# Two graph layers on one core: one-hot rows made from PSUM in halves, a base read once, and row constants in PSUM

## The chip, the core and the metric

The kernel runs on one core of a Trainium2 chip. The core has five engines with a queue each: PE (TensorE, matrix products), DVE (VectorE), ACT (ScalarE), POOL (GpSimd) and SP (which only issues transfers here). An engine works through its queue in the order in which the instructions were put there, and waits for others by semaphores. The metric is the device time of one execution in microseconds (us); the kernel before has a median of 2407.45 us over three runs (2405.77 to 2409.37).

## What is computed

A graph of 6250 nodes with 128 features and 106,250 edges, sorted by destination. Two layers, each on a layer norm of its input and added to it. The first is an attention layer, the second a gated message layer:

```python
# layer 0 (h = relu(layernorm(x)))
m = leaky_relu(xl[src] + xr[dst] + edge_attr @ We, 0.2)
logits = m @ att
alpha = softmax of logits over the edges of each dst
out = segment_sum(xl[src] * alpha, dst)          # then gelu, batch norm
# layer 1 (h = relu(layernorm(x)))
em = relu(layer_norm(concat(h[src], h[dst]) @ msg_w + msg_b))
msgs = segment_sum(em * edge_weight, dst) / counts
h_new = relu(layer_norm(concat(h, msgs) @ upd_w + upd_b))
x = x + gate * h_new + (1 - gate) * h
```

## The kernel before

The edges are padded to 128 x 832 and cut into 104 blocks of 1024, eight tiles of 128 edges each. The edges of one block reach at most 126 consecutive destinations (the kernel tests that first, and has another path for graphs of which it isn't true). So a block s has a *base*, its first destination, and a *window* of 126 node rows from there on.

**Tables and setup.** A first stage makes the tables xl_d and xr_d in DRAM, one row per node. Then `fast()` (from L740) makes small per-edge columns. `dl_b` holds each edge's destination minus its block's base, a bf16 row of 1024 numbers per block with one block per partition; it is written to DRAM as `dl_d` (L794).

**The edge loops.** Two loops over blocks, one per layer (L1020 and L1286), stand under a manual schedule: each engine's queue has the instructions in the order of the program. A round s of either loop does, in this order:

- `load` (L851): SP fetches the window of block s+2 (126 rows of xr_d or b_d) into one of three tiles W, and `dlb`, the block's row of dl_d repeated on all 128 partitions (L856, 256 KB). The row to start from comes from `base_of` (L762), which reads the base into a register of SP.
- POOL issues eight indirect gathers (L196), one per tile of 128 edges, for the source rows of block s: `gl`. The first loop has ten such buffers, the second six.
- `spread` / `spread1`: PE spreads the window of block s+1 over its edges (`expand`, L867: 16 matmul instructions, from the one-hot tile `oht`) into PSUM.
- DVE adds gl to the spread rows of block s (L1033, L1298), ACT goes on with the sum (L1034; squares at L1303).
- For an older block u (u = s-7 in the first loop, s-1 in the second) DVE makes the one-hot `oh` of destinations by edges (L1040, L1309), from `iota_ps`, a constant row 0..127 held in PSUM.
- First loop: ACT scales gl of block u by its softmax weights into `glw` (L1049); DVE goes on with block s (L1051 to L1057). Second loop: DVE scales y of block u by its reciprocal deviation and the row mg_r (L1314, eight instructions) and adds the row mb_r (L1316), both rows in SBUF; ACT does the relu (L1317) and the edge weights (L1320) into `glw`.
- `one_hot_t` (L861): DVE makes `oht` of block s+2 in one instruction from dlb (L863), 1 where the partition's number is the edge's offset.
- PE sums the edges of block u by destination, `agg` (L1063, L1329, 16 matmul instructions); ACT copies the sums out in the next round, and `store` (L869) has SP write them to the window's rows in DRAM, for which it reads the base again.

Around this, generators are taken one step further per round: in the first loop `maxima` (L896, softmax maxima of four blocks, whose small transposes share one PSUM buffer with the tag "mx") and `nodes` (L949), in the second `nodes1` (L1202), which finishes 512 nodes in eight steps, with transposes in PSUM buffers "nt" and "nz" (L1226 to L1228, L1236 to L1240, L1264 to L1273). After both loops a tail finishes the last nodes.

In PSUM the spread rows have two buffers; iota_ps, the sums and the two others of each loop (mx and np, nt and nz) have one each.

Of the kernel before, what the change touches and what calls it, by code (L numbers as in the profile page):

```python
# [9 lines left out]
F32 = mybir.dt.float32  # L10
BF16 = mybir.dt.bfloat16
# [5 lines left out]
P = 128  # L17
# [31 lines left out]
def kernel(  # L49
# [691 lines left out]
    def fast():  # L741
# [4 lines left out]
        fs = fx.enter_context(tc.tile_pool(name="fstate", bufs=1))  # L746
        a_d = dram.tile([NP, D], F32, name="a_d")
        b_d = dram.tile([NP + P, D], F32, name="b_d")
        dl_d = dram.tile([NS, SE], BF16, name="dl_d")
        res0_d = [dram.tile([NP + P, W0], F32, name=f"res0_{i}") for i in range(2)]  # L750
        res1_d = [dram.tile([NP + P, WL], F32, name=f"res1_{i}") for i in range(2)]
        hT_sb = h_sb.rearrange("p t f -> p (t f)")
        xT_sb = x_sb.rearrange("p t f -> p (t f)")

        dl_c = fs.tile([P, NS, ST], F32, name="dl_c")
        ew_c = fs.tile([P, NS, ST], F32, name="ew_c")
        eac_c = fs.tile([P, NS, ST], F32, name="eac_c")
        fst_c = fs.tile([P, NS, ST], F32, name="fst_c")
        base_row = fs.tile([1, NS], I32, name="base_row")
        nc.sync.dma_start(base_row, flat(dst, [[1, 1], [SE, NS]]))  # L760

        def base_of(s):  # L762
            return nc.values_load(base_row[0:1, s : s + 1], engines=[mybir.EngineType.SP],
                                  min_val=0, max_val=NP - 1)


        kbrk = fs.tile([NBT, BT, P + 1], BF16, name="kbrk")
# [17 lines left out]
        with tc.tile_pool(name="col1", bufs=1) as p1, tc.tile_pool(name="rows", bufs=2) as rp, tc.tile_pool(  # L785
            name="ps_p", bufs=2, space=PSUM
        ) as ps_p:
            base_f = p1.tile([NS, 1], F32, name="base_f")
            V.tensor_copy(base_f, dst_r[:, 0:1])
            fr = rp.tile([NS, SE], F32, name="fr", tag="rows")  # L790
            V.tensor_scalar(fr, dst_r, base_f, None, op0=ALU.subtract)
            dl_b = p1.tile([NS, SE], BF16, name="dl_b")
            V.tensor_copy(dl_b, fr)
            nc.sync.dma_start(dl_d, dl_b)  # L794

            for w in Ws:
                nc.scalar.dma_start(w[WIN : WIN + 1], We)
                nc.scalar.dma_start(w[WIN + 1 : P], flat(br, [[0, 1], [1, D]]))
            for o in ohts:
                V.memset(o, 1.0)  # L800
            ends_i = p1.tile([1, 2, K], I32, name="ends_i")
            nc.scalar.dma_start(ends_i[:, 0, :], flat(dst, [[1, 1], [P, K]]))
            nc.scalar.dma_start(ends_i[:, 1, :], flat(dst, [[1, 1], [P, K]], P - 1))
            ea_r = rp.tile([NS, SE], F32, name="ea_r", tag="rows")
            nc.sync.dma_start(ea_r, flat(edge_weight1, [[SE, NS], [1, SE]]))
            for c, vec in ((bias_c, bias_out), (bng_c, bn_gamma), (bnb_c, bn_beta)):
                nc.scalar.dma_start(c, flat(vec, [[1, P], [1, 1]]))
            nc.scalar.dma_start(gb_c, flat(gate_b, [[0, P], [1, 1]]))
# [12 lines left out]
            ew_r = rp.tile([NS, SE], F32, name="ew_r", tag="rows")  # L821
            nc.sync.dma_start(ew_r, flat(edge_weight, [[SE, NS], [1, SE]]))
            columns(ps_p, ew_c, ew_r, "ctp")


            V.memset(kbrk[:, :, 0:1], 0.0)
            V.memset(kbrk[:, :, P : P + 1], 0.0)
            HB = 7
            for b in range(0, BT, HB):
                n = min(HB, BT - b)  # L830
                dst_n = p1.tile([NBT, HB, P], I32, name="dst_n")
                nc.sync.dma_start(dst_n[:, :n, :], flat(dst, [[P, NBT], [P * NBT, n], [1, P]], b * P * NBT))
# [12 lines left out]
        def zero(tables, n, i):  # L845

            for r in tables:
                nc.sync.dma_start(r.rearrange("(p k) f -> p (k f)", p=P)[:, i * 5 * n : (i + 1) * 5 * n],
                                  zt[:, : 5 * n])

        def load(pool, table, s, weights):  # L851

            w, oht = Ws[s % 3], ohts[s % 3]
            nc.sync.dma_start(w[:WIN], table[ds(base_of(s), WIN), :])
            dlb = pool.tile([P, SE], BF16, name="dlb")
            nc.sync.dma_start(dlb, flat(dl_d, [[0, P], [1, SE]], s * SE))  # L856
            if weights:
                nc.sync.dma_start(oht[WIN : WIN + 1, :], flat(edge_weight1, [[SE, 1], [1, SE]], s * SE))
            return w, dlb, oht

        def one_hot_t(w, dlb, oht):  # L861

            V.tensor_scalar(oht[:WIN, :], dlb[:WIN, :], iota_p[:WIN, :], None, op0=ALU.is_equal)  # L863

        def expand(ps, oht, w):
            for j in range(ST):
# [1 line left out]

        def store(agg, tables, s):  # L869
            nc.sync.dma_start(tables[s % 2][ds(base_of(s), WIN), :], agg[:WIN, :])  # L870

        def fetch(fin, tables, t0, n):

# [12 lines left out]
        with tc.tile_pool(name="e0", bufs=2) as ep, tc.tile_pool(  # L886
# [1 line left out]
        ) as op_, tc.tile_pool(name="e0m", bufs=2) as mp, tc.tile_pool(name="e0n", bufs=1) as np_, tc.tile_pool(  # L888
            name="ps_m", bufs=2, space=PSUM
        ) as ps_m, tc.tile_pool(name="ps_1", bufs=1, space=PSUM) as ps_1, tc.manual_schedule():  # L890
            iota_ps = ps_1.tile([P, P], F32, name="iota_ps")
            S.copy(iota_ps, iota_f)
            LAG = SB + 3
            gls, lgc, exm, wins, pss, aggs = {}, {}, {}, {}, {}, {}

# [103 lines left out]
                S.copy(xT_sb[:, t0 * P : (t0 + n) * P], tp[:, : n * P])  # L999

            def spread(s):
                w, _, oht = wins.pop(s)
                pss[s] = ps_m.tile([P, ST, D], F32, name="m_ps")
                expand(pss[s], oht, w)

# [9 lines left out]
            for s in range(2):  # L1015
                wins[s] = load(op_, xr_d, s, True)
            for s in range(2):
                one_hot_t(*wins[s])
            spread(0)
            for s in range(NS + LAG + 1):  # L1020
                u = s - LAG
# [15 lines left out]
                if 0 <= u < NS:  # L1037
                    b, q = divmod(u, SB)
                    oh = ep.tile([P, ST, P], F32, name="oh")
                    V.tensor_tensor(oh, over_tiles(iota_ps, ST), over_features(dl_c[:, u, :], ST),  # L1040
                                    ALU.is_equal)
                    glw = ep.tile([P, ST, W0], F32, name="glw")
                    V.tensor_copy(glw[:, :, D:], exm[b][:, q])  # L1043
                if u >= 1:
                    flush(u - 1)
                if 0 <= u < NS:
# [9 lines left out]
                        lgc[s // SB] = mp.tile([P, SB, ST], F32, name="lgc")  # L1056
                    V.tensor_add(lgc[s // SB][:, s % SB, :], lr, eac_c[:, s, :])  # L1057
                if s + 2 < NS:
                    one_hot_t(*wins[s + 2])
                if 0 <= u < NS:  # L1060
                    aggs[u] = ps_1.tile([P, W0], F32, name="agg_ps")
                    for j in range(ST):
# [115 lines left out]
        with tc.tile_pool(name="e1g", bufs=6) as gp, tc.tile_pool(name="e1", bufs=2) as ep, tc.tile_pool(  # L1178
# [1 line left out]
        ) as yp, tc.tile_pool(name="e1o", bufs=2) as op_, tc.tile_pool(name="e1s", bufs=1) as e1, tc.tile_pool(  # L1180
            name="ps_m1", bufs=2, space=PSUM
        ) as ps_m, tc.tile_pool(name="ps_11", bufs=1, space=PSUM) as ps_1, tc.manual_schedule():
            iota_ps = ps_1.tile([P, P], F32, name="iota_ps1")
            S.copy(iota_ps, iota_f)
            glws = [e1.tile([P, ST, WL], F32, name=f"glw1_{i}") for i in range(3)]
            for t in glws:
                V.memset(t[:, :, D : D + 1], 1.0)
# [2 lines left out]
            wins, pss, aggs, rss, ys = {}, {}, {}, {}, {}  # L1190

            def spread1(s):
                w, _, oht = wins.pop(s)
                pss[s] = ps_m.tile([P, ST, D], F32, name="y_ps")
                expand(pss[s], oht, w)

# [84 lines left out]
            for s in range(2):  # L1281
                wins[s] = load(op_, b_d, s, False)
            for s in range(2):
                one_hot_t(*wins[s])
            spread1(0)
            for s in range(NS + 2):  # L1286
                u = s - 1
# [19 lines left out]
                if 0 <= u < NS:  # L1307
                    oh = ep.tile([P, ST, P], F32, name="oh1")
                    V.tensor_tensor(oh, over_tiles(iota_ps, ST), over_features(dl_c[:, u, :], ST),  # L1309
                                    ALU.is_equal)  # L1310
                    yu = ys.pop(u)
                    ru = rss.pop(u)
                    for j in range(ST):
                        V.scalar_tensor_tensor(yu[:, j, :], yu[:, j, :], ru[:, j : j + 1], mg_r,  # L1314
                                               op0=ALU.mult, op1=ALU.mult)
                    V.tensor_tensor(yu, yu, over_tiles(mb_r, ST), ALU.add)  # L1316
                    S.activation(yu, yu, AF.Relu)  # L1317
                    glw = glws[u % 3]
                    for j in range(ST):
                        S.activation(glw[:, j, :D], yu[:, j, :], AF.Copy, scale=ew_c[:, u, j : j + 1])  # L1320
                if s + 2 < NS:
                    one_hot_t(*wins[s + 2])
                if s < NS:
                    V.reciprocal(rs, rs)
                    rss[s] = rs
# [59 lines left out]
```

## Time and profile before

| what | us |
|---|---|
| median of three runs | 2407.45 |
| the profiled execution | 2414.23 |
| its span, first to last instruction | 2412.4 |
| gathers of the first loop | from 71.6 to 1145.7 |
| gathers of the second loop | from 1256.8 to 2355.2 |
| POOL busy | 1699.7 |
| DVE busy | 1637.3 |
| PE busy | 1375.8 |
| ACT busy | 1276.6 |

A line of a group gives the code line, the engine, the operation, the tile written and those read, the shapes, the number of instructions, and behind the bar the busy time and the mean of one in ns, then the idle time of the engine ahead of them and what ended it. A row of the timeline gives the start in us from the span's start, the duration, the engine, the line and the operation; several instructions in a row are merged ("x8"), and the idle time ahead of the first stands in brackets with what ended it. In the chain of what ended last, "issue" is time in which an engine waited for nothing that the profile shows. PE's ends are modelled, so neighbours may overlap by a tenth or two.

### The profile page before, as it was taken

How to read it: one execution, taken by the hardware profiler on the slowest of the kernel's cores; microseconds unless marked ns; L12 is line 12 of the kernel's file. 1: busy time of each engine (PE TensorE's matmuls, PEld its weight loads, DVE VectorE, ACT ScalarE, POOL GpSimd, SP SyncE). 2: the span in 40 equal slices, each digit the busy share in tenths (PEclk: the TensorE clock that was granted, in tenths of full speed). 3: DMA queues.
4: the chain of work that ended last, by engine and by line, in shares of the span. 5: the costliest groups of instructions: out<-in, count | busy, mean ns of one | idle time of the engine just before them, and what ended most of it. 6: DMA issues, size and time to landing. Idle time of an engine off the chain costs nothing.

```text
span 2412.4 us, 30614 instructions
## 1 busy us (share of the span) xinstructions
PE 1375.8 (57%) x7692; PEld 1270.8 (53%) x7692; DVE 1637.3 (68%) x3597; ACT 1276.6 (53%) x4267; POOL 1699.7 (70%) x1703
## 2 busy tenths in 40 slices
PE   6446555556566556565484555555655655555553
PEld 3345555555555455565464555555555654555553
DVE  6666677677677667767445567677767768768765
ACT  5223343334344334344456676676676677667663
POOL 1677777777777777777057777777777777777770
PEclk9667887787878777777687677778777777777876
DMA  6743455443443433443142333343333333333331
GB/s 166 211 114 92 111 151 137 98 100 92 101 100 92 98 96 92 100 100 80 32 132 79 90 94 99 85 107 97 83 107 97 85 108 103 83 101 102 85 96 30
DMA packets 217496, 242.90 MB, mean 101 GB/s; under 512 B 41373, under 2 KB 158077, under 8 KB 217309
## 3 DMA queue, kind: packets, MB, share of 16 engines
q0 software_dynamic: 53792, 110.57, 19.7%
q1 hardware_dynamic: 160657, 130.00, 18.5%
q8 instruction: 64, 1.05, 0.2%
q14 instruction: 123, 1.01, 0.1%
q10 hardware_dynamic: 2860, 0.27, 0.1%
HBM read 197.43 MB, written 43.25 MB: 100 GB/s over the span
## 4 chain that ended last, share of the span: by engine, by line
POOL 44%; issue 18%; DMA 14%; DVE 13%; PE 7%; ACT 3%; SPq 0%; DVEq 0%; another core or an unknown queue 0%; ACTq 0%; POOLq 0%
POOL gl L196 44%; DMA gl<-xl_d,src_c 7%; DMA gl<-a_d,src_c 5%; DVE y L1314 2%; DVE m_ps L1033 2%; PE agg_ps L1063 2%; DVE y L1298 1%; DVE oh L1309 1%; PE agg_ps L1329 1%; DVE y L1316 1%; PE mm L255 1%; PE mm L1156 1%; ACT sq L1303 1%; DVE oh L1040 1%; DVE oht L863 1%
## 5 line engine op out<-in xcount | busy, mean ns | idle before, releaser
L196 POOL DMA_INDIRECT gl<-xl_d,src_c x832 | 820.9, 987 | 308.8 <-issue 229.8
L196 POOL DMA_INDIRECT gl<-a_d,src_c x832 | 845.2, 1016 | 260.7 <-issue 234.3
L1329 PE MATMUL agg_ps<-glw,oh 128*128 128x129 f32 x1664 | 363.9, 403 | 485.7 <-ACT glw L1320 439.7
L1329 PEld LDWEIGHTS agg_ps<-glw,oh 128*128 128x128 f32 x1664 | 336.3, 298 | 505.8 <-ACT glw L1320 505.8
L1063 PE MATMUL agg_ps<-glw,oh 128*128 128x130 f32 x1664 | 345.0, 389 | 386.3 <-DVE glw L1043 206.8
L1063 PEld LDWEIGHTS agg_ps<-glw,oh 128*128 128x128 f32 x1664 | 320.7, 288 | 404.1 <-ACT glw L1049 404.1
L1034 ACT ACTIVATE m_ps<-m_ps 128x1024 f32<-128x1024 f32 x104 | 104.8, 1008 | 573.6 <-DVE m_ps L1033 429.3
L1303 ACT ACTIVATE sq<-y 128x128 f32<-128x128 f32 x832 | 257.1, 309 | 275.8 <-DVE y L1298 252.4
L1033 DVE TENSOR_TENSOR m_ps<-m_ps,gl 128x1024 f32<-128x1024 f32 x104 | 128.1, 1232 | 299.9 <-DMA gl<-xl_d,src_c 273.7
L867 PE MATMUL m_ps<-W,oht 128*128 128x128 f32 x1664 | 259.8, 320 | 36.2 <-DVE oht L863 22.8
L867 PEld LDWEIGHTS m_ps<-W,oht 128*128 128x128 f32 x1664 | 243.8, 233 | 45.2 <-issue 22.3
L1320 ACT ACTIVATE glw<-y,ew_c 128x128 f32<-128x128 f32 x832 | 254.4, 389 | 3.4
L1049 ACT ACTIVATE glw<-gl,exm 128x128 f32<-128x128 f32 x832 | 254.3, 394 | 0.0
L1298 DVE TENSOR_TENSOR y<-y_ps,gl 128x1024 f32<-128x1024 f32 x104 | 126.8, 1220 | 187.8 <-DMA gl<-a_d,src_c 146.7
L867 PE MATMUL y_ps<-W,oht 128*128 128x128 f32 x1664 | 230.4, 298 | 13.2 <-DVE oht L863 9.0
L867 PEld LDWEIGHTS y_ps<-W,oht 128*128 128x128 f32 x1664 | 226.7, 218 | 13.8 <-issue 13.8
L1314 DVE SCALAR_TENSOR_TENSOR y<-y,rs,mg_r 128x128 f32<-128x128 f32 x832 | 227.3, 344 | 0.0
L863 DVE TENSOR_SCALAR oht<-dlb,iota_p 126x1024 f32<-126x1024 bf16 x208 | 159.3, 766 | 15.1 <-DMA dlb<-dl_d 15.0
L1303 ACT ACTIVATION_READ_ACCUMULATOR sq<-y 128x1 f32 x832 | 155.0, 186 | 0.0
L1051 DVE TENSOR_TENSOR m_ps<-m_ps,att 128x1024 f32<-128x1024 f32 x104 | 131.3, 1263 | 4.8 <-ACT m_ps L1034 4.6
L1317 ACT ACTIVATE y<-y 128x1024 f32<-128x1024 f32 x104 | 109.9, 1057 | 41.1 <-DVE y L1316 41.0
L1316 DVE TENSOR_TENSOR y<-y,mb_r 128x1024 f32<-128x1024 f32 x104 | 127.7, 1228 | 3.6
(251 smaller groups left out, 1610.7 us busy)
## 6 DMA issues: line engine op xcount, KB each, us to landing
dlb<-dl_d SPq DMA_DIRECT2D x208, 256.0 KB
gl<-xl_d,src_c POOLq DMA_INDIRECT x832
gl<-a_d,src_c POOLq DMA_INDIRECT x832
res<-agg SPq DMA_DIRECT2D x104, 64.0 KB
res<-agg SPq DMA_DIRECT2D x104, 63.5 KB
W<-xr_d SPq DMA_DIRECT2D x104, 63.0 KB
W<-b_d SPq DMA_DIRECT2D x104, 63.0 KB
res<-zt SPq DMA_DIRECT2D x20, 325.0 KB
```

The costliest lines, as they stand in the source:

```text
L196: GP.indirect_dma_start(out=dest, out_offset=None, in_=table, in_offset=bass.IndirectOffsetOnAxis(ap=idx, axis=0))
L863: V.tensor_scalar(oht[:WIN, :], dlb[:WIN, :], iota_p[:WIN, :], None, op0=ALU.is_equal)
L867: T.matmul(ps[:, j, :], oht[:, j * P : (j + 1) * P], w, start=True, stop=True)
L1033: V.tensor_tensor(ps, ps, gl[:, :, :D], ALU.add)
L1049: S.activation(glw[:, j, :D], glu[:, j, :D], AF.Copy, scale=exm[b][:, q, j, 1:2])
L1063: T.matmul(aggs[u], oh[:, j, :], glw[:, j, :], start=(j == 0), stop=(j == ST - 1))
L1298: V.tensor_tensor(y, pss.pop(s), gl, ALU.add)
L1303: S.activation(sq, y[:, j, :], AF.Square, accum_out=rs[:, j : j + 1])
L1314: V.scalar_tensor_tensor(yu[:, j, :], yu[:, j, :], ru[:, j : j + 1], mg_r, op0=ALU.mult, op1=ALU.mult)
L1316: V.tensor_tensor(yu, yu, over_tiles(mb_r, ST), ALU.add)
L1320: S.activation(glw[:, j, :D], yu[:, j, :], AF.Copy, scale=ew_c[:, u, j : j + 1])
L1329: T.matmul(aggs[u], oh[:, j, :], glw[:, j, :], start=(j == 0), stop=(j == ST - 1))
```

## The change

Three things, in one diff.

1. The offsets `dl_b` stay in SBUF; dl_d and the load of dlb are gone. `one_hot_t` now works on half a block (512 edges): PE multiplies a column of the identity, repeated 128 times (it picks the block's row of dl_b), with the half row, which puts the offsets on all partitions in a PSUM tile `dlp`; DVE makes the half of oht from it. dlp takes the one buffer "mx" in the first loop and "nt" in the second. The first half is put ahead of the older work of the round: in the first loop after the one-hot oh and the copy at L1043, in the second between L1309 and L1314. The second half stands where the one instruction stood.
2. The base of a block is read into SP's register once, and kept until `store`.
3. A helper `constants` puts rows into one PSUM tile: iota in the first loop, as before; iota, mg_r and mb_r in the second, where L1314 and L1316 read them from there.

```diff
+        dl_b = fs.tile([NS, SE], BF16, name="dl_b")
+        ident_b = fs.tile([P, P], BF16, name="ident_b")
+        V.tensor_copy(ident_b, ident)
...
+        bases = {}
+
         def base_of(s):
-            return nc.values_load(base_row[0:1, s : s + 1], engines=[mybir.EngineType.SP],
-                                  min_val=0, max_val=NP - 1)
+            if s not in bases:
+                bases[s] = nc.values_load(base_row[0:1, s : s + 1], engines=[mybir.EngineType.SP],
+                                          min_val=0, max_val=NP - 1)
+            return bases[s]
...
-            dl_b = p1.tile([NS, SE], BF16, name="dl_b")
             V.tensor_copy(dl_b, fr)
-            nc.sync.dma_start(dl_d, dl_b)
...
+        def constants(pool, *rows_):
+
+            n = 1 + len(rows_)
+            t = pool.tile([P, n * P], F32, name="cst")
+            for k, r in enumerate((iota_f,) + rows_):
+                S.copy(t[:, k * P : (k + 1) * P], r)
+            return [t[:, k * P : (k + 1) * P] for k in range(n)]
+
         def load(pool, table, s, weights):
 
             w, oht = Ws[s % 3], ohts[s % 3]
             nc.sync.dma_start(w[:WIN], table[ds(base_of(s), WIN), :])
-            dlb = pool.tile([P, SE], BF16, name="dlb")
-            nc.sync.dma_start(dlb, flat(dl_d, [[0, P], [1, SE]], s * SE))
             if weights:
                 nc.sync.dma_start(oht[WIN : WIN + 1, :], flat(edge_weight1, [[SE, 1], [1, SE]], s * SE))
-            return w, dlb, oht
-
-        def one_hot_t(w, dlb, oht):
-
-            V.tensor_scalar(oht[:WIN, :], dlb[:WIN, :], iota_p[:WIN, :], None, op0=ALU.is_equal)
+            return w, oht
+
+        def one_hot_t(pool, tag, s, k, w, oht):
+
+            es = slice(k * CH, (k + 1) * CH)
+            dlp = pool.tile([P, CH], F32, name="dlp", tag=tag)
+            T.matmul(dlp, ident_b[:NS, s : s + 1].to_broadcast([NS, P]), dl_b[:, es], start=True, stop=True)
+            V.tensor_scalar(oht[:WIN, es], dlp[:WIN, :], iota_p[:WIN, :], None, op0=ALU.is_equal)
```

The first loop:

```diff
             for s in range(2):
-                one_hot_t(*wins[s])
+                for k in range(2):
+                    one_hot_t(ps_1, "mx", s, k, *wins[s])
...
                     V.tensor_copy(glw[:, :, D:], exm[b][:, q])
+                if s + 2 < NS:
+                    one_hot_t(ps_1, "mx", s + 2, 0, *wins[s + 2])
                 if u >= 1:
                     flush(u - 1)
...
                 if s + 2 < NS:
-                    one_hot_t(*wins[s + 2])
+                    one_hot_t(ps_1, "mx", s + 2, 1, *wins[s + 2])
```

The second loop:

```diff
-            iota_ps = ps_1.tile([P, P], F32, name="iota_ps1")
-            S.copy(iota_ps, iota_f)
+            iota_ps, mg_ps, mb_ps = constants(ps_1, mg_r, mb_r)
...
                     V.tensor_tensor(oh, over_tiles(iota_ps, ST), over_features(dl_c[:, u, :], ST),
                                     ALU.is_equal)
+                if s + 2 < NS:
+                    one_hot_t(ps_1, "nt", s + 2, 0, *wins[s + 2])
+                if 0 <= u < NS:
                     yu = ys.pop(u)
                     ru = rss.pop(u)
                     for j in range(ST):
-                        V.scalar_tensor_tensor(yu[:, j, :], yu[:, j, :], ru[:, j : j + 1], mg_r,
+                        V.scalar_tensor_tensor(yu[:, j, :], yu[:, j, :], ru[:, j : j + 1], mg_ps,
                                                op0=ALU.mult, op1=ALU.mult)
-                    V.tensor_tensor(yu, yu, over_tiles(mb_r, ST), ALU.add)
+                    V.tensor_tensor(yu, yu, over_tiles(mb_ps, ST), ALU.add)
...
                 if s + 2 < NS:
-                    one_hot_t(*wins[s + 2])
+                    one_hot_t(ps_1, "nt", s + 2, 1, *wins[s + 2])
```

More of the change, by code (lines that the diff above doesn't have):

```diff
@@ L748, in fast @@
         b_d = dram.tile([NP + P, D], F32, name="b_d")
-        dl_d = dram.tile([NS, SE], BF16, name="dl_d")
         res0_d = [dram.tile([NP + P, W0], F32, name=f"res0_{i}") for i in range(2)]
@@ L870, in store @@
             nc.sync.dma_start(tables[s % 2][ds(base_of(s), WIN), :], agg[:WIN, :])
+            del bases[s]
         def fetch(fin, tables, t0, n):
@@ L890, in fast @@
         ) as ps_m, tc.tile_pool(name="ps_1", bufs=1, space=PSUM) as ps_1, tc.manual_schedule():
-            iota_ps = ps_1.tile([P, P], F32, name="iota_ps")
-            S.copy(iota_ps, iota_f)
+            (iota_ps,) = constants(ps_1)
             LAG = SB + 3
@@ L1001, in spread @@
             def spread(s):
-                w, _, oht = wins.pop(s)
+                w, oht = wins.pop(s)
                 pss[s] = ps_m.tile([P, ST, D], F32, name="m_ps")
@@ L1182, in fast @@
         ) as ps_m, tc.tile_pool(name="ps_11", bufs=1, space=PSUM) as ps_1, tc.manual_schedule():
-            iota_ps = ps_1.tile([P, P], F32, name="iota_ps1")
-            S.copy(iota_ps, iota_f)
+            iota_ps, mg_ps, mb_ps = constants(ps_1, mg_r, mb_r)
             glws = [e1.tile([P, ST, WL], F32, name=f"glw1_{i}") for i in range(3)]
@@ L1192, in spread1 @@
             def spread1(s):
-                w, _, oht = wins.pop(s)
+                w, oht = wins.pop(s)
                 pss[s] = ps_m.tile([P, ST, D], F32, name="y_ps")
@@ L1283, in fast @@
             for s in range(2):
-                one_hot_t(*wins[s])
+                for k in range(2):
+                    one_hot_t(ps_1, "nt", s, k, *wins[s])
             spread1(0)
```

## The prediction, made before the change was run

> **What bounds the kernel now.** I read the page first (busy shares, the chain that ended last, the costliest groups), then the spread of the gathers' durations, then the timeline of one round of each edge loop.
>
> ```profile
> span 2412.4 us, 30614 instructions
> PE 1375.8 (57%) x7692; PEld 1270.8 (53%) x7692; DVE 1637.3 (68%) x3597; ACT 1276.6 (53%) x4267; POOL 1699.7 (70%) x1703
> POOL 44%; issue 18%; DMA 14%; DVE 13%; PE 7%; ACT 3%; SPq 0%; DVEq 0%; another core or an unknown queue 0%; ACTq 0%; POOLq 0%
> L863 DVE TENSOR_SCALAR oht<-dlb,iota_p 126x1024 f32<-126x1024 bf16 x208 | 159.3, 766 | 15.1 <-DMA dlb<-dl_d 15.0
> ```
> ```profile
> L196 POOL DMA_INDIRECT gl<-xl_d,src_c x832: 940/944/1701, 71.6 to 1144.8; - x167
> L196 POOL DMA_INDIRECT gl<-a_d,src_c x832: 940/945/1954, 1256.8 to 2354.3; - x167
> ```
> The chain is mostly POOL's gathers and the 0.305 us between two of them ("issue"). 832 x (0.944 + 0.305) = 1039 us for a loop, 9.99 us for a round of eight; the loops' gathers take 1074 and 1098 us. POOL never waits for a buffer in either loop: its gaps are all 0.3 us. The rest is stretch: 820.9 - 832 x 0.944 = 35.5 us in the first loop, 845.2 - 785.4 = 59.8 in the second.
>
> ```profile
> 1517.74 1.74 POOL L196 DMA_INDIRECT gl<-a_d,src_c  x1 [0.30 <-issue]
> 1518.58 0.74 DVE L863 TENSOR_SCALAR oht<-dlb,iota_p 126x1024 f32<-126x1024 bf16 x1
> ```
> The gather that meets the one-hot of L863 ends 0.16 us after it, 0.80 late. Laying POOL's rows on DVE's: gathers over 0.96 us that overlap an L863 hold 30.2 us of the first loop's stretch and 48.6 of the second's; those that overlap only L1314 or L1316 hold 9.6.
>
> The other clock is the hand-over between engines. One round of the second loop and the head of the next:
>
> ```profile
> 1502.07 1.23 DVE L1298 TENSOR_TENSOR y<-y_ps,gl 128x1024 f32<-128x1024 f32 x1 [5.02 <-DMA gl<-a_d,src_c]
> 1503.21 1.21 DVE L1309 TENSOR_TENSOR oh<-iota_ps,dl_c 128x1024 f32<-128x1024 f32 x1
> 1504.35 2.18 DVE L1314 SCALAR_TENSOR_TENSOR y<-y,rs,mg_r 128x128 f32<-128x128 f32 x8
> 1506.56 1.22 DVE L1316 TENSOR_TENSOR y<-y,mb_r 128x1024 f32<-128x1024 f32 x1
> 1507.70 0.75 DVE L863 TENSOR_SCALAR oht<-dlb,iota_p 126x1024 f32<-126x1024 bf16 x1
> 1507.82 1.06 ACT L1317 ACTIVATE y<-y 128x1024 f32<-128x1024 f32 x1 [0.56 <-DVE y L1316]
> 1508.91 2.45 ACT L1320 ACTIVATE glw<-y,ew_c 128x128 f32<-128x128 f32 x8
> 1509.36 3.81 PE L1329 MATMUL agg_ps<-glw,oh 128*128 128x129 f32 x16 [7.27 <-ACT glw L1320]
> 1512.96 2.62 PE L867 MATMUL y_ps<-W,oht 128*128 128x128 f32 x16
> 1512.95 1.23 DVE L1298 TENSOR_TENSOR y<-y_ps,gl 128x1024 f32<-128x1024 f32 x1 [0.83 <-DMA gl<-a_d,src_c]
> 1515.22 2.18 DVE L1314 SCALAR_TENSOR_TENSOR y<-y,rs,mg_r 128x128 f32<-128x128 f32 x8
> ```
> See: each queue runs in program order, and the spread of the next window (L867) comes right behind the segment sums (L1329). Its result is first used by the L1298 of the round after, so today the ring STT (L1314) -> relu -> weights -> sums -> spread -> L1298 closes over two rounds. In the 1512.95 round DVE goes straight on from L1309 to L1314 while PE still spreads until 1515.6.
>
> **The change, part by part.**
> *Load of destinations gone:* 208 transfers of 256 KB, SP issues of 0.34 us, and the dl_d write. W and the gathers have the DMA engines at 35 to 43%, and POOL doesn't wait for landings: 0. L863's 15.0 us wait for dlb goes; DVE then waits for the gather instead (256 and 138 us of such waits): 0. If the cover were gone, 15 us.
> *Base read once:* a register read less on SP per round. SP's longest waits are for the flushed sums, it has no work late: 0; at worst a few tenths per round on a queue that idles most of it.
> *One-hot from PSUM:* two halves of 512 for one of 1024. No row shows a tensor-scalar of 512 from PSUM. From below, half of L863's 0.66 start-to-start, 0.33; from above, L984's scalar-tensor-tensor of 512 from PSUM, 0.744, of which the next instruction overlaps 0.08: 0.66. I take 0.66, the row with the same source. DVE: +0.66 per round, on 742 us busy in 1050 (99 rounds: 7.5 each); 8.2 is under 9.99, so alone it costs nothing.
> *Stretch:* L863 covers 1024 elements in the 0.74 us that L984 takes for 512 from PSUM. If the slow kind of one-hot leaves the gathers alone, as L984 and L1033 mostly do, POOL gets back 30.2 + 48.6, and 9.6 for mg_r and mb_r moved to PSUM, if POOL stays the bound. That last term is where a rule and the rows differ. The Trainium skill's "SBUF — State Buffer", section "Who interferes with whom", has a DVE instruction with two SBUF inputs contend with GpSimd work that reads SBUF, and the second to issue blocked in full. By it, gathers issued during L1314 and L1316 (3.4 us of each round) would lose some 1 us per round, an estimate of 100 us in place of the 9.6; the rows decide, at about 0.08 us per gather met.
> *Two spreading matmuls per round, "dlp":* bf16, 512 columns. No row has one: from below, a 128-column f32 pass issued every 0.122 us (1.95/16 in L867), from above L1126's f32 pass of 512, 0.665. I take 0.4.
> *Constants:* two ACT copies more (L1199's size, 0.25) at the head of the second loop, none in the first: under 1 us, ahead of waits for the first gather.
>
> *The wait it adds.* In the second loop the first half is put between L1309 and L1314. On PE its dlp stands behind spread1(s+1), which stands behind the segment sums of the round before. On DVE, L1314, L1316 and the second half are queued behind it, and ACT's relu and weights and PE's sums wait for those. The ring now closes in one round:
> first half 0.66; L1314 to L1316 2.21; to relu 1.26; to weights 1.09; to sums 0.45 (all start to start, medians); sums' start to spread's end 5.9; dlp 0.4; total 11.97, say 12.0 us against POOL's 9.99. The 5.9: in the 69 rounds with nothing between the two it has median 5.71 and mean 5.51; the first twelve rounds average 6.06, and their PE idles 4 to 5 us ahead of the sums, as it will here.
> From y(0) at 1268.8 to y(103) at 2360.1 now: 1091 us. After: 103 x 12.0 = 1236.
> Eleven node groups lie inside. Their DVE and ACT work fits into the 4.8 us that DVE then idles per round (12.0 less 7.2 of work), but three steps put work between sums and spread, or between it and DVE's next half: the transposes at L1228 0.8 (0.77 at 1438.92); L1236/L1237 1.8 on PE, and then DVE's L1240, L1298, L1309 end 5.3 after the sums instead of 2.5: 2.8; L1268 to L1273, 4.9 instead of 2.5: 2.4. 6.0 x 11 = 66.
> Second loop: 1236 + 66 - 1091 = +211. POOL runs five rounds ahead and waits for buffers.
>
> In the first loop the same insertion is harmless: the weights (L1049) come from a gather seven rounds old, not through the half. Ring: half 0.75, second dlp 0.5, sums 3.8, a maximum's transposes 0.3, spread 2.2, dlp 0.4: 8.0, under 9.99; a round with L975 and L982 about 2.5 more, made up in two rounds; POOL has ten buffers for a lag of seven. So POOL keeps the pace and gains its 30.2.
>
> Sum: 2414.2 (profiled execution: span 2412.4 and 1.8 around it) - 30 + 211 = 2595. The median of the runs is 6.8 lower: 2588.
>
> **The rivals.**
> 1. *The ring doesn't bind; faster.* If the half got its dlp early, POOL would bound both loops: 2407.5 - 30.2 - 58.2 = 2319. For it: POOL 70% busy, and the 8.2 us of DVE work. Against: PE's order above. It decides at a ring of 10.24 us (103 x 10.24 + 66 = 1091 + 30): sums to spread's end would have to fall to 4.2; the shortest of the 69 is 4.3.
> 2. *The ring binds in both loops.* With dlp 0.67, spread 2.9 and sums at 3.8 the first loop's ring is 9.4 and node rounds carry it over 9.99: gain gone and 30 to 50 us added: 2588 + 30 + 40 = 2658.
> 3. *PSUM frees nothing.* Gathers stretch as before by the halves: the first loop keeps its 30, the second is ring-bound anyway: 2618.
> 4. *A quick ring.* Half 0.33, dlp 0.12, sums to spread 5.5: 11.0; 103 x 11.0 + 40 - 1091 = +82: 2459.
>
> **How the numbers follow.** My case 0.66, rival 2 0.08, rival 3 0.07, rival 4 and its neighbours 0.13, rival 1 0.06. My case's own range is 2530 to 2640 (ring 11.5 to 12.5). Eight in ten, with rivals 2 and 3 and the upper half of 4: 2490 to 2660. About 0.2% is what a measurement can tell from no change: faster 0.05, same 0.01 (both rival 1, partly), slower 0.94.
>
> **What would show it.** Right: in the second loop POOL's gaps name a wait for DVE's y, DVE's new one-hot waits 4 to 5 us for PE in each round, L1298 comes every 12 us; in the first loop gathers end near 1115 with few over 1 us. Wrong: rounds of 10 us in the second loop (rival 1), DVE waiting for PE in the first (rival 2), 1.7 us gathers still there (rival 3). I would be most wrong if PE's spread didn't stand behind the sums.

## The result, and the profile after

The changed kernel takes 2586.22 us (median of 4 runs, 2583.19 to 2587.83), the kernel before beside it 2408.41 (4 runs): ratio 1.0738, 95% interval 1.0719 to 1.0756. The profiled execution has a span of 2582.3 us and a time of 2584.67. Forecast were 2588 and a slower kernel.

The lines of the page that answer to those shown of before: span, busy time of the engines, the chain of work that ended last, and the one-hot's group (out<-in, count | busy, mean ns of one | idle before it, with its releaser).

```profile
span 2582.3 us, 30444 instructions
PE 1489.7 (58%) x8108; PEld 1297.8 (50%) x8108; DVE 1761.6 (68%) x3806; ACT 1277.3 (49%) x4269; POOL 1610.4 (62%) x1703
PE 26%; DVE 25%; POOL 24%; issue 11%; DMA 7%; ACT 6%; SPq 0%; DVEq 0%; another core or an unknown queue 0%; ACTq 0%; POOLq 0%
L876 DVE TENSOR_SCALAR oht<-dlp,iota_p 126x512 f32<-126x512 f32 x416 | 309.5, 744 | 360.7 <-PE dlp L875 360.7
```

POOL's share of the chain falls from 44% to 24%. PE, DVE and ACT, 23% together before, hold 57%: the chain now goes round between them. POOL's busy time fell, 1699.7 to 1610.4 us, and no other engine is near full. A kernel that gets slower while its bound has less to do, and nothing else fills up, is to be searched for a ring of waits: engines that wait for one another in a circle, so that a round can't begin before the last one has gone all the way round.

The gathers by line (shortest, median, longest in ns; first and last start), and three lines of the list of waits (total, times, longest, in us):

```profile
L196 POOL DMA_INDIRECT gl<-xl_d,src_c x832: 940/945/1663, 71.6 to 1114.3; - x167
L196 POOL DMA_INDIRECT gl<-a_d,src_c x832: 938/945/1369, 1229.9 to 2467.9; - x167
```
```profile
PE agg_ps L1348 <- ACT glw L1339: 462.8, 104, 6.5
DVE oht L876 <- PE dlp L875: 360.7, 122, 5.9
POOL gl L196 <- DVE y L1314: 208.7, 35, 9.7
```

The first loop's gathers start last at 1114.3 for 1144.8 before: it got 30.5 us faster. The second loop's take 1239 us for 1098, and POOL, which never waited for a buffer before, waits 208.7 us for DVE's y. Laid end to end, with the add that makes y (L1314, L1298 before) as the mark: first y of the second loop 27.6 us earlier (1241.2 for 1268.8), first to last y 1289.9 us for 1091.3 (+198.6), behind the last y 51.3 for 52.3. That is -27.6 + 198.6 - 1.0 = +170.0, and the spans differ by 169.9.

One round of the second loop in the timeline (start, duration, engine, line; in brackets idle time and what ended it), DVE, then PE, then ACT; the rows that don't bear on the ring are left out:

```profile
1853.40 0.75 DVE L876 TENSOR_SCALAR oht<-dlp,iota_p 126x512 f32<-126x512 f32 x1 [2.01 <-PE dlp L875]
1854.06 2.15 DVE L1333 SCALAR_TENSOR_TENSOR y<-y,rs,cst 128x128 f32<-128x128 f32 x8
1856.25 1.22 DVE L1335 TENSOR_TENSOR y<-y,cst 128x1024 f32<-128x1024 f32 x1
1858.15 1.17 DVE L1314 TENSOR_TENSOR y<-y_ps,gl 128x1024 f32<-128x1024 f32 x1
1859.24 1.21 DVE L1325 TENSOR_TENSOR oh<-cst,dl_c 128x1024 f32<-128x1024 f32 x1
1865.28 0.75 DVE L876 TENSOR_SCALAR oht<-dlp,iota_p 126x512 f32<-126x512 f32 x1 [4.82 <-PE dlp L875]
```
```profile
1859.04 3.76 PE L1348 MATMUL agg_ps<-glw,oh 128*128 128x129 f32 x16 [4.46 <-ACT glw L1339]
1862.64 0.60 PE L1243 MATMUL nt<-ident,fin 128*128 128x128 f32 x4
1863.07 1.95 PE L880 MATMUL y_ps<-W,oht 128*128 128x128 f32 x16
1864.86 0.38 PE L875 MATMUL dlp<-dl_b,ident_b 104*128 104x512 bf16 x1
```
```profile
1857.50 1.06 ACT L1336 ACTIVATE y<-y 128x1024 f32<-128x1024 f32 x1 [3.28 <-DVE y L1335]
1858.59 2.44 ACT L1339 ACTIVATE glw<-y,ew_c 128x128 f32<-128x128 f32 x8
```

DVE's half (L876) stands ahead of L1333; relu (L1336) and weights (L1339) wait for L1335, the sums (L1348) for the weights, the spread (L880) stands behind the sums, the matmul that makes the next half's input (L875) behind the spread, and the next half starts 11.88 us after this one. DVE sits idle 4.82 us ahead of it, PE 4.46 us ahead of the sums: two engines waiting in turn for each other. (The four transposes at L1243 belong to a node group; they stand in this round between the sums and the spread.)

### The profile page after: what moved, and what is told of

Its sections match the earlier page's. It is cut to its first block, busy times and chain, and to the rows that moved or that the text cites. A ratio compares the mean times of both kernels' runs of the same rounds, so it can differ in the third digit from the quotient of the medians.

```text
span 2582.3 us, 30444 instructions
## 1 busy us (share of the span) xinstructions
PE 1489.7 (58%) x8108; PEld 1297.8 (50%) x8108; DVE 1761.6 (68%) x3806; ACT 1277.3 (49%) x4269; POOL 1610.4 (62%) x1703
## 4 chain that ended last, share of the span: by engine, by line
PE 26%; DVE 25%; POOL 24%; issue 11%; DMA 7%; ACT 6%; SPq 0%; DVEq 0%; another core or an unknown queue 0%; ACTq 0%; POOLq 0%
POOL gl L196 24%; PE agg_ps L1348 13%; DVE y L1333 7%; PE y_ps L880 6%; DMA gl<-xl_d,src_c 5%; DVE y L1335 4%; ACT y L1336 4%; DVE oht L876 3%; DVE m_ps L1047 2%; ACT glw L1339 2%; DVE y L1314 1%; DVE oh L1325 1%; PE agg_ps L1079 1%; PE mm L1172 1%; PE mm L255 1%
## 5 line engine op out<-in xcount | busy, mean ns | idle before, releaser
L196 POOL DMA_INDIRECT gl<-a_d,src_c x832 | 786.2, 945 | 460.0 <-issue 232.4
L196 POOL DMA_INDIRECT gl<-xl_d,src_c x832 | 790.5, 950 | 308.1 <-issue 234.9
L1348 PEld LDWEIGHTS agg_ps<-glw,oh 128*128 128x128 f32 x1664 | 361.9, 329 | 652.1 <-ACT glw L1339 652.1
L1348 PE MATMUL agg_ps<-glw,oh 128*128 128x129 f32 x1664 | 389.9, 427 | 462.8 <-ACT glw L1339 462.8
L876 DVE TENSOR_SCALAR oht<-dlp,iota_p 126x512 f32<-126x512 f32 x416 | 309.5, 744 | 360.7 <-PE dlp L875 360.7
L875 PE MATMUL dlp<-dl_b,ident_b 104*128 104x512 bf16 x416 | 172.4, 414 | 442.8 <-DVE oht L876 310.4
L1079 PE MATMUL agg_ps<-glw,oh 128*128 128x130 f32 x1664 | 299.4, 354 | 21.9 <-ACT glw L1065 16.2
L1336 ACT ACTIVATE y<-y 128x1024 f32<-128x1024 f32 x104 | 109.9, 1057 | 323.7 <-DVE y L1335 323.7
L1339 ACT ACTIVATE glw<-y,ew_c 128x128 f32<-128x128 f32 x832 | 254.5, 389 | 3.4
L880 PEld LDWEIGHTS y_ps<-W,oht 128*128 128x128 f32 x1664 | 246.8, 235 | 8.4 <-issue 6.7
L880 PE MATMUL m_ps<-W,oht 128*128 128x128 f32 x1664 | 246.9, 310 | 5.9 <-DVE lr L1069 5.9
L880 PE MATMUL y_ps<-W,oht 128*128 128x128 f32 x1664 | 248.2, 313 | 0.0
L880 PEld LDWEIGHTS m_ps<-W,oht 128*128 128x128 f32 x1664 | 230.8, 222 | 15.6 <-DVE lr L1069 11.0
L1333 DVE SCALAR_TENSOR_TENSOR y<-y,rs,cst 128x128 f32<-128x128 f32 x832 | 223.2, 341 | 0.0
L1314 DVE TENSOR_TENSOR y<-y_ps,gl 128x1024 f32<-128x1024 f32 x104 | 124.7, 1199 | 20.5 <-DMA gl<-a_d,src_c 19.5
L1069 DVE TENSOR_REDUCE lr<-m_ps 128x8 f32<-128x1024 f32 x104 | 127.4, 1225 | 3.6
```

The costliest lines, as they stand in the source:

```text
L196: GP.indirect_dma_start(out=dest, out_offset=None, in_=table, in_offset=bass.IndirectOffsetOnAxis(ap=idx, axis=0))
L875: T.matmul(dlp, ident_b[:NS, s : s + 1].to_broadcast([NS, P]), dl_b[:, es], start=True, stop=True)
L876: V.tensor_scalar(oht[:WIN, es], dlp[:WIN, :], iota_p[:WIN, :], None, op0=ALU.is_equal)
L880: T.matmul(ps[:, j, :], oht[:, j * P : (j + 1) * P], w, start=True, stop=True)
L1079: T.matmul(aggs[u], oh[:, j, :], glw[:, j, :], start=(j == 0), stop=(j == ST - 1))
L1348: T.matmul(aggs[u], oh[:, j, :], glw[:, j, :], start=(j == 0), stop=(j == ST - 1))
```

## The experiments

My theory: the new half one-hot in front of the second loop's normalization closes a ring of 12 us, and everything else in the change costs nothing or gains. Against it stood a wider rival, that DVE's added work or its new instructions themselves cost the time, and open was which part frees POOL.

**The half moved, nothing else.** In the second loop the first half goes behind L1335 and the weights, next to the second half. Same instructions, same count.

```diff
-                if s + 2 < NS:
-                    one_hot_t(ps_1, "nt", s + 2, 0, *wins[s + 2])
-                if 0 <= u < NS:
                     yu = ys.pop(u)
...
                 if s + 2 < NS:
-                    one_hot_t(ps_1, "nt", s + 2, 1, *wins[s + 2])
+                    for k in range(2):
+                        one_hot_t(ps_1, "nt", s + 2, k, *wins[s + 2])
```


> The changed kernel with the first half's one-hot of the second loop moved behind the row constants (L1335) and the weights, next to the second half; nothing else. Theory (the ring through the first half sets the second loop's pace): the half no longer stands ahead of L1333, the ring closes over two rounds at about 7.5 us each, POOL sets the pace at 9.99 us again and keeps what it won: about 2407 - 30 - 58 = 2319 us, gathers of the second loop within 1045 us. Rival (the halves from PSUM cost what they cost by their work on DVE and PE, wherever they stand): 2560 to 2590 us.

Measured: 2327.45 us against 2417.61, ratio 0.9626 (0.9604 to 0.9649). The move alone turns 7% slower into 4% faster; this version beats both kernels. The gathers of its second loop, and part of a round on DVE and PE:

```profile
L196 POOL DMA_INDIRECT gl<-a_d,src_c x832: 940/944/1442, 1223.8 to 2263.4; - x167
```
```profile
1737.65 2.15 DVE L1330 SCALAR_TENSOR_TENSOR y<-y,rs,cst 128x128 f32<-128x128 f32 x8
1739.83 1.22 DVE L1332 TENSOR_TENSOR y<-y,cst 128x1024 f32<-128x1024 f32 x1
1740.96 0.74 DVE L876 TENSOR_SCALAR oht<-dlp,iota_p 126x512 f32<-126x512 f32 x1
```
```profile
1734.01 3.75 PE L1346 MATMUL agg_ps<-glw,oh 128*128 128x129 f32 x16 [0.28 <-ACT glw L1336]
1738.04 1.95 PE L880 MATMUL y_ps<-W,oht 128*128 128x128 f32 x16
```

The normalization (L1330 here) starts at 1737.65, before PE has begun the spread (1738.04); it no longer waits for it, so the ring spans two rounds again. Second loop: 1040 us from first to last gather, 832 x (0.944 + 0.305) = 1039. POOL is the bound, and the stretch (what its gathers take beyond 832 x 0.944 us) is only 1.9 us.

**A delay in the ring, and one beside it.** The 1.2-us one-hot of the segment sums is written a second time, once right ahead of the half and once between L1333 and the add. Equal work; only the first place can hide in the 4.8 us that DVE waits.

```diff
                     V.tensor_tensor(oh, over_tiles(iota_ps, ST), over_features(dl_c[:, u, :], ST),
                                     ALU.is_equal)
+                    V.tensor_tensor(oh, over_tiles(iota_ps, ST), over_features(dl_c[:, u, :], ST),
+                                    ALU.is_equal)
                 if s + 2 < NS:
                     one_hot_t(ps_1, "nt", s + 2, 0, *wins[s + 2])
```


> The changed kernel with the one-hot of L1325 made twice in each round of the second loop, the second time right behind the first, ahead of the first half: 1.13 us more DVE work per round. Theory (ring): DVE waits 4 to 5 us for PE at that place, so plain rounds don't move; only the two node rounds per group in which DVE comes last pay, 22 x 1.13 = 25 us, 2611. Rival (DVE's work sets the second loop's pace): 104 x 1.13 = 117 us, 2703.

```diff
                         V.scalar_tensor_tensor(yu[:, j, :], yu[:, j, :], ru[:, j : j + 1], mg_ps,
                                                op0=ALU.mult, op1=ALU.mult)
+                    V.tensor_tensor(oh, over_tiles(iota_ps, ST), over_features(dl_c[:, u, :], ST),
+                                    ALU.is_equal)
                     V.tensor_tensor(yu, yu, over_tiles(mb_ps, ST), ALU.add)
```


> The changed kernel with the same second L1325 per round, but between L1333 and L1335, behind the first half. Theory (ring): it lies on the ring in every round, 103 x 1.13 = 116 us, 2702. Rival (DVE's work sets the pace): the same 117 us as when it stands ahead; so the two kernels together tell. If POOL or the gathers set the pace: 0.

Measured: 2609.28 (ratio 1.079, 1.0757 to 1.0823) ahead of the half and 2731.42 (1.1295, 1.126 to 1.1329) behind it; the changed kernel has 1.0738. The second loop's gathers, first with the work ahead of the half, then behind it:

```profile
L196 POOL DMA_INDIRECT gl<-a_d,src_c x832: 938/944/1362, 1228.3 to 2490.3; - x167
L196 POOL DMA_INDIRECT gl<-a_d,src_c x832: 938/944/1065, 1228.7 to 2603.1; - x167
```

In the traces the 101 periods from one round's first half to the next sum to 1268.0 us in the changed kernel, 1292.1 with the work ahead of the half, 1410.2 with it behind. So 1.2 us per round costs 24 us in one place and 142 in the other (12.5 and 134 by the ratios): the ring is shown, and DVE's load alone is not the cause. The 142 is more than the 101 x 1.02 = 103 of the delay itself (L1333 to the add, start to start, 2.18 to 3.20 us). Nearly all of the other 39 lies on PE: from the sums' start to the spread's end it takes 6.42 us instead of 6.06 in the mean of the rounds without node work, and 101 x 0.37 = 37. PE's granted clock from 1260 to 2200 us is 0.68 there, against 0.73 in the changed kernel and 0.82 with the half moved: on these three PE idles longer the slower the ring, and its clock is lower. That the one causes the other is argued, not shown.

**The first loop alone.** It has the changed first loop, and the second loop of before with its load, its one one-hot per block and its rows in SBUF; the base is still read once.

```diff
             for s in range(2):
-                one_hot_t(*wins[s])
+                for k in range(2):
+                    one_hot_t(ps_1, "mx", s, k, *wins[s])
...
-                    for k in range(2):
-                        one_hot_t(ps_1, "nt", s + 2, k, *wins[s + 2])
+                    one_hot_2(*wins[s + 2])
```
(the first hunk stands against the kernel before, the second against the half moved)

> The change in the first loop alone; the second loop as before (offsets loaded from DRAM, one one-hot of 1024, row constants in SBUF). Theory: POOL sets the first loop's pace and gets its 30 us of stretch back, 98.75% of the kernel before, 2385 where that takes 2415. Rival (the first loop pays for the early half as the second does): no gain or slower.

> The changed first loop with the second loop of before (its load of destinations, its one one-hot per block, mg_r and mb_r in SBUF). The kernel first_loop_only once more: it ran on a chip where the kernel before took 2994 us. Theory (the loss is the second loop's ring alone; in the first loop the insertion is harmless and the gathers gain 30 us): ratio 0.9875, first-loop gathers end near 1113, second loop as before. Rival (the first loop's half, put ahead of the sums, costs something too, as 1.0235 on the other chip would have it): ratio above 1.01 here as well, first-loop gathers ending later than before's 1145.7, with POOL waiting for ACT's weights.

The first of these two ran on a chip that is told of below. The second: 2386.74 us against 2417.32, ratio 0.9871 (0.9839 to 0.9902), expected 0.9875. Its gathers:

```profile
L196 POOL DMA_INDIRECT gl<-xl_d,src_c x832: 940/944/1969, 69.2 to 1111.3; - x167
L196 POOL DMA_INDIRECT gl<-a_d,src_c x832: 940/944/1998, 1227.8 to 2329.6; - x167
```

The first loop gives its 31 us (1042.1 us from first to last gather for 1073.2), and the second takes 1102 us for 1097 before. So the whole loss is the second loop's.

**Slack of the first loop.** The 1.2-us one-hot written twice there, in the changed kernel (the diff is that of the first delay, at L1054).

> The changed kernel with the one-hot oh of the first loop (L1054) made twice in each round, ahead of the first half: 1.13 us more DVE work on the way to it. Theory (the first loop's ring is 8.0 us, POOL's pace 9.99): up to 10 us in node rounds, else nothing: 2586 to 2596. Rival (the first loop is at its ring or at DVE too): 90 to 117 us.

Measured: ratio 1.0716 (1.0688 to 1.0745), that is 2 us over the changed kernel by the medians, nothing by the ratios. There DVE has room for at least another 1.2 us in each round.

**Which part frees POOL?** First only the rows: the kernel before, with mg_r and mb_r in PSUM.

```diff
-            iota_ps = ps_1.tile([P, P], F32, name="iota_ps1")
-            S.copy(iota_ps, iota_f)
+            iota_ps, mg_ps, mb_ps = constants(ps_1, mg_r, mb_r)
...
-                    V.tensor_tensor(yu, yu, over_tiles(mb_r, ST), ALU.add)
+                    V.tensor_tensor(yu, yu, over_tiles(mb_ps, ST), ALU.add)
```


> The kernel before with one part of the change alone: mg_r and mb_r copied to PSUM and read from there in the second loop. Theory by the rows of before: the 9.6 us of stretch that gathers take next to L1314 and L1316, 2398. Rival, by the SBUF page's rule: about 100 us, 2308. No effect: 2407.

Then the reverse: the half moved, and the two rows back in SBUF.

```diff
-                        V.scalar_tensor_tensor(yu[:, j, :], yu[:, j, :], ru[:, j : j + 1], mg_ps,
+                        V.scalar_tensor_tensor(yu[:, j, :], yu[:, j, :], ru[:, j : j + 1], mg_r,
                                                op0=ALU.mult, op1=ALU.mult)
-                    V.tensor_tensor(yu, yu, over_tiles(mb_ps, ST), ALU.add)
+                    V.tensor_tensor(yu, yu, over_tiles(mb_r, ST), ALU.add)
```


> The kernel with the late half, with mg_r and mb_r read from SBUF again. Theory by the rows of before (gathers that met only L1314 or L1316 held 9.6 us of stretch): 10 us slower than the late half. Rival, by the rule of the skill's SBUF page (the second to issue is blocked in full): about 100 us slower. If the reading of stretch is wrong altogether: no difference.

Measured: 2372.49 against 2414.31 (ratio 0.9827, 0.9809 to 0.9845), 42 us gained by moving two rows; and 2378.23 against 2327.45 on the same chip, 51 us lost by moving them back. In the traces the second loop's stretch falls from 59.8 to 17.8 us in the first case and rises from 1.9 to 56.3 in the second. Both are far from the 10 us that I had read from the rows. The rows in SBUF once more, gathers and DVE:

```profile
1706.18 1.06 POOL L196 DMA_INDIRECT gl<-a_d,src_c  x1 [0.30 <-issue]
1708.85 1.48 POOL L196 DMA_INDIRECT gl<-a_d,src_c  x1 [0.30 <-issue]
```
```profile
1706.08 2.18 DVE L1330 SCALAR_TENSOR_TENSOR y<-y,rs,mg_r 128x128 f32<-128x128 f32 x8
1708.29 1.23 DVE L1332 TENSOR_TENSOR y<-y,mb_r 128x1024 f32<-128x1024 f32 x1
1709.43 0.75 DVE L876 TENSOR_SCALAR oht<-dlp,iota_p 126x512 f32<-126x512 f32 x1
```

The second gather starts 0.56 us into L1332, which ends at 1709.52, and ends at 1710.33, 0.81 after. The first starts 0.10 into the first of the eight short instructions of L1330 (0.34 us each), and ends 0.82 after that one. A gather takes 0.944 us undisturbed, so it looks as if it needs something about 0.13 us after its start, and gets it only when a DVE instruction that began before it is over.

The trace of before, sorted by this signature (the DVE instruction that the end of a late gather, one of over 0.96 us, follows by 0.79 to 0.84 us, or for L863 also by 0.10 to 0.135), gives another split than my prediction's: in its second loop L1316 holds 45.0 us of the stretch, L1314 8.4, and L863 4.6; in its first loop L863 holds 30.5 of 35.5.

**The one-hot as a two-input instruction.** In the kernel before, L863 takes iota as a second tile operand instead of a scalar.

```diff
-            V.tensor_scalar(oht[:WIN, :], dlb[:WIN, :], iota_p[:WIN, :], None, op0=ALU.is_equal)
+            V.tensor_tensor(oht[:WIN, :], dlb[:WIN, :], iota_p[:WIN, :].to_broadcast([WIN, SE]), ALU.is_equal)
```


> The kernel before with L863 as an instruction of two inputs (offsets and the partition's number spread over the columns) in place of one input and a scalar; load, place and PE's work as before. Theory (gathers are held up by the fast kind of one-hot from SBUF, 1024 elements in 0.75 us): it takes 1.2 us instead of 0.75, the 79 us of stretch next to it go, and some 0.08 us per gather met come back as next to L1316, 17 us: 2407 - 62 = 2345. Rival (any one-hot of this size that writes SBUF holds POOL up): no gain, or slower by DVE's 0.5 us per round.

I was wrong: 2464.68, ratio 1.0205 (1.0186 to 1.0224), 50 us lost. I had taken the fast kind of one-hot for the cause and two SBUF inputs for harmless.

```profile
604.01 1.22 DVE L863 TENSOR_TENSOR oht<-dlb,iota_p 126x1024 f32<-126x1024 bf16 x1
```
```profile
604.11 1.93 POOL L196 DMA_INDIRECT gl<-xl_d,src_c  x1 [0.30 <-issue]
```

The one-hot ends at 605.23, the gather at 606.04, 0.81 later, and this one loses almost 1 us. In its first loop the two-input one-hot holds 66.0 of 71.3 us of stretch. Over both loops the stretch is 143.0 us for 95.3 before: that is 48 of the 50 us, so they are not DVE's longer work.

**The load left out**, for all blocks but the first two. The one-hots are then those of wrong blocks; the work and its order stay.

```diff
-            dlb = pool.tile([P, SE], BF16, name="dlb")
-            nc.sync.dma_start(dlb, flat(dl_d, [[0, P], [1, SE]], s * SE))
+            dlb = dlbs[s % 2]
+            if s < 2 and weights:
+                nc.sync.dma_start(dlb, flat(dl_d, [[0, P], [1, SE]], s * SE))
```


> The kernel before with the load of dlb left out for all blocks but the first two of the first loop (two tiles that stay, so the one-hots are those of wrong blocks; work and order as before). Theory: the 53 MB were hidden, POOL keeps the pace and its stretch: 2407, within 5 us. Rival (the traffic slows the gathers, or their stretch comes from it): faster by over 20 us.

Measured: ratio 1.0023 (1.001 to 1.0036). By DMA go 188.84 MB for 242.90, and nothing is gained; the load was hidden.

**The base read twice again**, on the version with the half moved.

```diff
-            if s not in bases:
-                bases[s] = nc.values_load(base_row[0:1, s : s + 1], engines=[mybir.EngineType.SP],
-                                          min_val=0, max_val=NP - 1)
-            return bases[s]
+            return nc.values_load(base_row[0:1, s : s + 1], engines=[mybir.EngineType.SP],
+                                  min_val=0, max_val=NP - 1)
```


> The kernel with the late half, with the base read twice per block again, by the load and by the store. Theory: SP has time, no difference: 96.26% of the kernel before, as the late half alone. Rival (a second read per round stands in the way of the loads or stores): more than 97%.

> The kernel late_half with the block's base read twice, as before the change. The kernel late_half_two_reads once more, for the same reason. Theory (SP's queue has no work that is late, so the read costs nothing): ratio 0.9626, as late_half. Rival (a register read on SP holds back the loads or the stores of the sums): some tenths of a us per round, so 20 us in each loop and a ratio near 0.98.

The second of these: 2328.53 us, ratio 0.9632 (0.9602 to 0.9662), against 0.9626 with one read. The read costs nothing.

**The other chip.** The first run of the last kernel and of the first loop alone came to a chip on which the kernel before took 2994.42 us (9 runs, 2981.84 to 2996.84). There the ratios were 1.0743 (1.0714 to 1.0773) and 1.0235 (1.0208 to 1.0263), and they answer none of the questions above. What stands out in the trace is SP's queue. One of its register moves, by line, on that chip and then on the chip of the second run (shortest, median, longest in ns):

```profile
L864 SPq MOVE W<-xr_d x104: 3/29/708, 76.2 to 1505.1; - x104
```
```profile
L864 SPq MOVE W<-xr_d x104: 29/29/38, 74.2 to 1089.7; - x104
```

The median is the same and the longest 708 ns. Of the kernel's 420 moves 66 take over 0.4 us there, and none in the second run. In such a stretch SP starts an instruction every 1.4 us (from 138 to 150 us, for one), and DVE, PE and ACT then stand, while POOL's gathers go on: DVE waits 45.6 us ahead of one half, by the profile for something that it can't name. DVE's own instructions last as long as elsewhere. That SP's queue is what they wait for is read from this coincidence, not shown; and what slows it in these stretches is open.

## Why the prediction was right, and where it was not

- *The ring (12.0 us per round).* Right, term by term in medians: half 0.667 (0.66 said), L1333 to the add 2.18 (2.21), to relu 1.25 (1.26), to weights 1.09 (1.09), to sums 0.45 (0.45), sums' start to spread's end 5.91, mean 6.06 (5.9). The last, dlp, was mis-sized: from the spread's modelled end to the half's start 0.26, not 0.4; the matmul's row reads 0.38 and begins before the spread's last row ends. The 70 rounds without node work have mean 11.95, median 11.81.
- *Node work (6.0 per group).* Right: transposes +0.5, the two matmul groups +2.8 each, 6.1.
- *Second loop, y to y: 1302 us.* Measured 1289.9. My 103 x 12.0 + 66 had small excesses that add up: 101 periods of 11.95 for 12.0 (5 us), 61 us of node work for 66 (5), and two rounds at the ends, where no half follows, of 21.9 for 24 (2). That is 12 us too much on +211.
- *First loop, -30.* Right (-30.5), and for the reason given: L863's effect on the gathers is gone (stretch 35.5 to 5.1 us), and the inserted half binds nothing.
- *The sum.* 2595 for the profiled execution, 2584.67 measured; taking 6.8 off for the median brought it to 2588, but this time the profiled execution lay 1.5 under the median. The two errors, 10 and 8 us, cancelled: a miss of 2 us is finer than the working was.
- *Load and base: 0.* Right, each by a run of its own.
- *Stretch: 48.6 on L863 and 9.6 on L1314 and L1316 in the second loop.* This step failed. The total was right (the half moved gains 90 us against before, by the prediction's rival 1 some 88), so the time was not touched; the split was nearly the reverse. I put a late gather down to any L863 that it overlapped, and L863 runs right behind L1316. The pair that I quoted had a third row in the same view, which I had not set beside it:

```profile
1517.44 1.22 DVE L1316 TENSOR_TENSOR y<-y,mb_r 128x1024 f32<-128x1024 f32 x1
```

The gather ends at 1519.48, that is 0.16 after L863's end, but also 0.82 after the end of L1316, which began 0.30 before the gather, and 0.82 is the number that recurs.
- *The rule that I set aside.* The Trainium skill's "SBUF — State Buffer", section "Who interferes with whom", says that a DVE instruction with two SBUF inputs contends with GpSimd work that reads SBUF. The runs agree on that: 42 us gained, 51 lost by the two rows. My estimate of 100 us from it was about twice too large: in the trace of before L1316 holds 73 gathers, for 0.62 us in the mean, but L1314 is eight short instructions, and the 109 gathers that it holds wait for one of them, 0.08 us each. The same section says of tensor_tensor that it did not stall DMAs that GpSimd issues; here L863 in that form held up gathers for 66.0 us of one loop, and the measurement decides.
- *Signs.* As named: POOL's gaps name DVE's y, the new half waits for PE (360.7 us in all, 331 of it in the second loop, 4.82 in the round shown), the first loop's gathers end near 1115. "In each round" was too much: 80 of the second loop's 102 first halves wait. A sign of rival 2 came too: in the first loop 34 of the inserted halves wait for PE, 26 us in all and 2.6 at most. It cost nothing, since POOL's gathers kept their pace.

Of the rivals, the second falls with the first loop's gathers, the third with the stretch of 0.8 us left in the second loop's, the fourth with the periods. Rival 1, a free ring, is what the half moved makes of it: 2327 measured, 2319 worked out; the kernel before beside it took 2418 there, 9 more than beside the changed kernel.

## What to carry to other kernels

Before you put an instruction into an in-order queue, follow what it waits for back to the instruction it holds up; if the two meet, add up the whole ring, start to start, and set it against the round of the bound. Where it is longer, move the instruction behind the work that others wait for: here the same instructions, behind the normalization instead of ahead of it, were worth 10%. And put a stall down to an instruction by a constant distance between their ends, not by overlap: neighbours in a queue tend to overlap the same thing.

## What the runs showed of the hardware that I had not expected

- An indirect gather on POOL is held up at two points. If a DVE instruction with two SBUF inputs, or the fast one-hot of L863, began before the gather and still runs about 0.13 us after the gather's start, the gather ends 0.82 us after that instruction (0.818 and 0.815 in the median). It matters which began first: in the first loop of before, 76 gathers started just ahead of or during an L863 that ran on so long; the 67 that started 0.092 us or more into it were held, the 9 others (0.077 or less) were not. For the two-input one-hot the line lies near 0.04 us. The second point is near the gather's end: an L863 that began 0.12 to 0.44 us into the gather makes it end 0.118 us after L863 (26 gathers of that loop); one that began 0.50 us into it or later doesn't, and two-input instructions don't show this second point.
- Operands moved to PSUM remove nearly all of both: with the rows and the one-hot's input there, the second loop's stretch is 1.9 us for 59.8.
- How many gathers are met depends on phase: with the rows in PSUM and L863 left as it was, L863's share of the second loop's stretch rose from 4.6 to 15.6 us, since L1316 no longer held the gathers ahead of it.
- One chip ran the kernel before 24% slower, the two versions traced there show SP's queue slow in stretches, and their sign was another there than on the chip of their second run. A ratio from one chip is not a property of the kernel until the kernel before runs there as it does elsewhere.
